# Four-layer graph network on one core: row-tile pairs of the second sweep set twice as far apart, and the last rows stored in one transfer from ScalarE's queue

## The chip, the cores and the metric

The kernel runs on one core of one Trainium2 chip. The metric is the device time of one execution in microseconds (us). Before the change it is 2903.23 us, the median of three runs (2901.61 to 2905.91). The profiled execution has a span of 2899.2 us.

## What is computed

Four layers of a graph network, each followed by a residual and a layer norm. `x` is 2708 x 512, `adj` is a sparse-valued but densely stored 2708 x 2708 matrix with non-negative entries. Cut to what matters here:

```python
deg = jnp.maximum((adj != 0).astype(jnp.float32).sum(-1), 1.0)
x = _layernorm(x + _L0_gnn_ref(x, adj))                    # weighted mean over neighbours
x = _layernorm(x + _L1_gnn_ref(x, adj, adj, ...))          # attention and a plain convolution
x = _layernorm(x + _L2_gnn_ref(x, adj, L2_gnn_weight))     # three hops
x = _layernorm(x + _L3_gnn_ref(x, adj, deg[..., None], L3_gnn_W, L3_gnn_b))

def _L1_gnn_ref(x, adj_a, adj_b, W_sa, a_sa, W_gcnb, b_gcnb, Wa, ba, Wb, bb):
    ...
    x_b = adj_b @ (x @ W_gcnb) + b_gcnb                    # the second sweep
    return jax.nn.sigmoid(attn_a * x_a + attn_b * x_b)

def _L3_gnn_ref(x, adjacency, node_degree, W, b):
    a_hat = adjacency + jnp.eye(n)
    dinv = jax.lax.rsqrt(node_degree)
    pooled = (dinv * a_hat * dinv) @ x + x
    return jax.nn.relu(pooled @ W + b)                     # dinv * dinv is 1 / degree, by rows
```

## The kernel before

Seven sweeps over the adjacency matrix make up the kernel; each is a product of `adj` with 512 columns of features. Products are cut into two halves in each direction and done with seven block products instead of eight (P1 to P7). `at(pos, fn)` puts a piece of work into a list at a position, and the list is emitted in the order of positions; a scheduler then lays out the instructions of each engine with this order as priority. In a sweep over `RANGES` a step of 1.0 is one block product, and a range takes seven steps.

```python
RANGES = [(0, 384), (384, 384), (768, 256), (1024, 330)]
PLAIN = dict(P1=0, P7=1, P5=2, P6=3, P4=4, P3=5, P2=6)      # where each block product starts
RING = 38
...
    def bank(nm, shape=None):                               # eight PSUM banks for everything
        return psum.tile(shape or [P, D], F32, name=nm, tag="x", bufs=8)
...
    def move(queue, dst, src):                              # rows in a multiple of 16, then the others
        m = dst.shape[0]
        c = m - m % 16 if m > 16 else m
        queue.dma_start(out=dst[:c], in_=src[:c])
        if c < m:
            queue.dma_start(out=dst[c:m], in_=src[c:m])
```

In the second sweep the rows of a finished range go through a dense product with `W_gcnb`, again in seven block products, tile by tile. `seven` does it in two parts. Part 0 fills the blocks u, c and d of two PSUM banks, and VectorE adds u, c and d to the outputs. Part 1 fills a and accumulates further products into u, c and d, so it has to wait until VectorE has read what part 0 left there.

```python
    def seven(part, Y, wop, H, lo, w, outs, scales, bases):
        if part == 0:
            x, y = bank("ps_7"), bank("ps_7")
            H.update(u=x[:, :HD], c=x[:, HD:], d=y[:, :HD], a=y[:, HD:])
        for home, a, v in SEV[part]:                        # three homes in part 0, four in part 1
            for c in range(2):
                nc.tensor.matmul(H[home][:w], Y[a, c][:, lo : lo + w], wop(v, c), ...)   # L644
        def acc(i, e, home, first=False):
            ...
                nc.vector.tensor_tensor(o, H[home][:w], b, ALU.add)                      # L651
        if part == 0:
            acc(0, 0, "u", True)
            acc(1, 1, "c", True)
            acc(1, 1, "d")
        else:
            acc(0, 0, "a")
            for i, e in ((1, 1), (0, 1), (1, 0)):
                acc(i, e, "u", (i, e) != (1, 1))
            acc(1, 0, "c")
            acc(0, 1, "d")
...
        # in done1, for every range but the last; p0 is step 7.12 of the range,
        # which is step 0.12 of the next one
        at(p0 + 0.3, lambda: Y.update(row_sums(...)))       # six new tiles of the ring
        for i, (t, lo, w) in enumerate(tiles):              # 3, 3 and 2 tiles of 128 rows
            ...
            at(p0 + 0.6 + 0.56 * i, lambda f=b7: f(0))
            at(p0 + 0.6 + 0.56 * i + 0.26, lambda f=b7: f(1))
```

While this happens, the next range runs: its block products (L457), the sums of adjacency tiles that they read (L402), the count of the degrees (L963), with `end(1)` (bank `ds`) at step 2.6 and `rows(1)` (bank `ps_r`) at step 3.2, and the attention scores (L900 to L916).

The last layer ends with `done6`. For the last group of rows it handles six tiles in a row, the last of them with 83 rows:

```python
            def b(s=s, lo=lo, w=w, r0=r0, got=got):
                px = dense(lambda c: cc(s, c)[:, lo : lo + w], W[6], w)                        # L605
                y = got["x"]
                ...
                nc.vector.scalar_tensor_tensor(px[:w], px[:w], rdeg_f[...], vec[6][:w], ...)   # L1479
                nc.vector.scalar_tensor_tensor(y[:w], px[:w], 0.0, y[:w], ALU.max, ALU.add)    # L1480
                layernorm([(y, 0, D)], y, w, True)          # L554 to L564, its end on ScalarE
                move(nc.sync, out[h * NH + r0 : h * NH + r0 + w, :], y[:w])                    # L151, L153
```

Of the kernel before, what the change touches and what calls it, by code (L numbers as in the profile page):

```python
# [27 lines left out]
NH = 1354  # L28
# [40 lines left out]
def gnn_kernel(ctx: ExitStack, tc: tile.TileContext, x, adjT, w_sa, a_sa, w_gcn, b_gcn, wab, bab, w_hop, w_out,  # L69
               b_out, out):  # L70
    nc = tc.nc
# [75 lines left out]
    def move(queue, dst, src):  # L147
# [6 lines that stand above are left out]
# [7 lines left out]
    def trans(nm):  # L161
        return pool.tile([P, 384], F32, name=nm, tag="ring", bufs=RING)

    def nat(nm):
        return pool.tile([P, D], F32, name=nm, tag="nat", bufs=6)
# [4 lines left out]
    def bank(nm, shape=None):  # L170
        return psum.tile(shape or [P, D], F32, name=nm, tag="x", bufs=8)
# [6 lines left out]
    def at(pos, fn, hold=False):  # L178

        def go():  # L180
            n = len(nc.cur_bb.bb.instructions)
            fn()
            held.update(range(n, len(nc.cur_bb.bb.instructions)))

        events.append((pos, len(events), go if hold else fn))
# [413 lines left out]
    def dense(lhs, wts, w):  # L599
        ps = bank("ps_d")  # L600
        for c in range(DC):
            for n in range(len(wts) // DC):
                r = wts[c] if len(wts) == DC else wts[2 * c + n]
                o = ps[:w] if len(wts) == DC else ps[:w, n * HD : (n + 1) * HD]
                nc.tensor.matmul(o, lhs(c), r, start=c == 0 and n == 0, stop=c == DC - 1, skip_group_check=True)  # L605
        return ps
# [16 lines left out]
    def row_sums(A, n):  # L623

        Y = {("A11", c): A[0, c] for c in range(2)}
        Y.update({("A12", c): A[0, 2 + c] for c in range(2)})
        Y.update({("A22", c): A[1, 2 + c] for c in range(2)})
        for c in range(2):
            for m, a, b, op in (("S3", A[0, c], A[1, c], ALU.subtract), ("S1", A[1, c], A[1, 2 + c], ALU.add),
                                ("S2", None, A[0, c], ALU.subtract), ("S4", A[0, 2 + c], None, ALU.subtract)):  # L630
                Y[m, c] = A[1, c] if m == "S1" else ring_tile("d7")
                a = Y["S1", c] if a is None else a
                b = Y["S2", c] if b is None else b
                nc.vector.tensor_tensor(Y[m, c][:, :n], a[:, :n], b[:, :n], op)
        return Y
# [6 lines that stand above are left out]
        for home, a, v in SEV[part]:  # L642
            for c in range(2):
                nc.tensor.matmul(H[home][:w], Y[a, c][:, lo : lo + w], wop(v, c),  # L644
                                 start=part == 0 and home in "ud" and c == 0, stop=c == 1, skip_group_check=True)

        def acc(i, e, home, first=False):
            o = outs[i][:w, e * HD : (e + 1) * HD]
            b = bases[i][:w, e * HD : (e + 1) * HD] if first else o
            if scales is None:  # L650
                nc.vector.tensor_tensor(o, H[home][:w], b, ALU.add)  # L651
            else:
                nc.vector.scalar_tensor_tensor(o, H[home][:w], scales[i], b, ALU.mult, ALU.add)
# [11 lines that stand above are left out]
# [182 lines left out]
    for k in range(KW):  # L847
        f = k / KT
# [89 lines left out]
    i = 0  # L938
# [55 lines left out]
    def done1(p0, dp, last, R0, n, h, C, tiles):  # L994
        Z = {}

        def gates():

            pg = bank("pg")
            for c in range(DC):  # L1000
                nc.tensor.matmul(pg[32 * c : 32 * c + 32, :n], wab_pad[:, c, :], C[h, c][:, :n], start=True, stop=True)
            Z[0] = trans("zg")
            nc.scalar.copy(Z[0][:, :n], pg[:, :n])

        def gate_tile(i, t, lo, w):
            if i == 0:
                Z[1] = bank("pz", [P, 8])
            pz = Z[1][:, 2 * i : 2 * i + 2]
            nc.tensor.matmul(pz[:w], Z[0][:, lo : lo + w], pick, start=i == 0, stop=True, skip_group_check=True)
            nc.vector.tensor_tensor(gate[:w, t, :], pz[:w], gate_x[:w, t, :], ALU.add)  # L1010
            nc.scalar.activation(gate[:w, t, :], gate[:w, t, :], AF.Sigmoid)

        def finish(t, w, y):
            nc.scalar.mul(y[:w], y[:w], gate[:w, t, 1:2])
            move(nc.gpsimd, XB[t], y[:w])

        at(p0 + 0.05, gates)
        for i, (t, lo, w) in enumerate(tiles):
            def b(i=i, t=t, lo=lo, w=w):
                gate_tile(i, t, lo, w)  # L1020
                if not last:
                    return
                px = dense(lambda c: C[h, c][:, lo : lo + w], W[1], w)
                y = nat("y")
                nc.vector.tensor_tensor(y[:w], px[:w], vec[1][:w], ALU.add)
                finish(t, w, y)

            at(p0 + 0.25 + (dp * i if last else 0.02 * i), b)
        if last or h:
            return  # L1030

        Y = {}
        at(p0 + 0.3, lambda: Y.update(row_sums({(i, c): C[1 - i, c] for i in range(2) for c in range(DC)}, n)))
        for i, (t, lo, w) in enumerate(tiles):
            H, y = {}, []

            def b7(part, t=t, lo=lo, w=w, H=H, y=y):
                if part == 0:
                    y.extend(nat("y") for _ in range(2))
                seven(part, Y, W[8], H, lo, w, y, None, [vec[1], vec[1]])  # L1040
                if part == 1:
                    for j in range(2):
                        finish(t + KT * (1 - j), w, y[j])

            at(p0 + 0.6 + 0.56 * i, lambda f=b7: f(0))
            at(p0 + 0.6 + 0.56 * i + 0.26, lambda f=b7: f(1))

    sweep(S[1], RANGES, extra=extra1, done=done1, late=0.85, save=True)

    eps_col = const.tile([P, NT], F32, name="eps_col")  # L1050
# [112 lines left out]
    def fetch2(src, h, r0, w):  # L1163
        o = nat("ld")
        for t, a, b, m in split(h, r0, w):
            move(nc.gpsimd, o[b : b + m, :], src[t][a : a + m, :])
        return o
# [297 lines left out]
    def done6(p0, dp, g, i0, n, h, cc, tiles):  # L1465

        end = (g, h) == (1, 0)
        for i, (s, lo, w) in enumerate(tiles[3:] + tiles[:3] if end else tiles):
            got = {}
            r0 = i0 + s * n + lo  # L1470

            def a(r0=r0, w=w, got=got):
                got["x"] = fetch2(X3, h, r0, w)

            def b(s=s, lo=lo, w=w, r0=r0, got=got):
                px = dense(lambda c: cc(s, c)[:, lo : lo + w], W[6], w)
                y = got["x"]
                r = 12 * g + 6 * h + 3 * s + lo // P
                nc.vector.scalar_tensor_tensor(px[:w], px[:w], rdeg_f[:w, r : r + 1], vec[6][:w], ALU.mult, ALU.add)  # L1479
                nc.vector.scalar_tensor_tensor(y[:w], px[:w], 0.0, y[:w], ALU.max, ALU.add)  # L1480
                layernorm([(y, 0, D)], y, w, True)
                move(nc.sync, out[h * NH + r0 : h * NH + r0 + w, :], y[:w])

            p = p0 - 0.095 + 0.14 * i if end else p0 + 0.1 + 0.28 * i
            at(p - 0.6, a)
            at(p, b)
# [57 lines left out]
```

## Time and profile before

| | |
|---|---|
| time, median of 3 runs | 2903.23 us |
| span of the profiled execution | 2899.2 us |
| VectorE busy | 2241.0 us (77%) |
| GpSimd busy | 626.6 us (22%) |
| mean DMA rate | 176 GB/s |
| second sweep | about 500 to 900 us |
| dense product of the second sweep (L644) | 554.0 to 788.3 us, 224 instructions of 0.379 us |
| last matrix product ends | about 2888.6 us |

Engines have short names in the profile: PE is TensorE's matrix product, PEld its loading of weights, DVE is VectorE, ACT ScalarE, POOL GpSimd, SP SyncE; a q behind a name means the engine's queue of orders. L644 is line 644 of the kernel. A line of a timeline gives the start, the length, the engine, the line, the operation, the tiles out and in, the shape and the number of instructions merged in it; brackets at its end hold the idle time before it and what ended it. A row of waits gives who waited, for what, how long in total, how often and the longest. A single-precision product shows as two instructions.

### The profile page before, as it was taken

Reading aid. Unit: us, or ns where it says so; the run is one execution under the profiler, and the core shown is the slowest. Engines: PE = TensorE matmul, PEld = TensorE weight load, DVE = VectorE, ACT = ScalarE, POOL = GpSimd, SP = SyncE. Lnnn points to the kernel's source line nnn. Section 1 sums busy time; section 2 is a strip of 40 time slices with the busy share of each in tenths; the row PEclk is TensorE's granted clock in tenths of the full one; section 3 lists DMA queues with packets and bytes.
Section 4 is the critical chain, followed back from the end, with each engine's and each line's share of the span. In section 5 each row is a group of like instructions: output and inputs, shape, how many; then the busy total and the mean of one; then the engine's idle time right before and its main releaser. Section 6 shows DMA issues by size and latency. Waiting matters only on the chain. (4 is left out here: it accounts for less than half of the span.)

```text
span 2899.2 us, 37366 instructions
## 1 busy us (share of the span) xinstructions
PE 2844.7 (98%) x10847; PEld 1852.6 (64%) x10847; DVE 2241.0 (77%) x5778; ACT 566.7 (20%) x1110; POOL 626.6 (22%) x1133
## 2 busy tenths in 40 slices
PE   7999999999999999999999999999999999999998
PEld 5655665657765656866666666666666666665664
DVE  6898798577748675875689788887888878798776
ACT  4544200001137454651100000000000100100001
POOL 0123224123310101122213033030330212501102
PEclk9999999999999999999999999999999999999999
DMA  7666466354544333564667667566675665764551
GB/s 228 190 211 180 132 211 228 108 173 152 172 150 128 118 115 96 171 197 151 202 208 226 204 197 235 171 205 204 198 234 167 196 187 171 237 172 142 173 154 59
DMA packets 373145, 511.50 MB, mean 176 GB/s; under 512 B 64022, under 2 KB 326096, under 8 KB 372940
## 3 DMA queue, kind: packets, MB, share of 16 engines
q1 hardware_dynamic: 307128, 372.01, 44.1%
q0 software_dynamic: 50272, 127.29, 12.9%
q10 hardware_dynamic: 15540, 9.82, 1.2%
q8 instruction: 86, 1.41, 0.2%
q14 instruction: 119, 0.97, 0.1%
HBM read 425.22 MB, written 83.67 MB: 176 GB/s over the span
## 5 line engine op out<-in xcount | busy, mean ns | idle before, releaser
L1218 DVE TENSOR_TENSOR z<-z 128x339 f32<-128x339 f32 (+1 forms) x966 | 456.0, 505 | 11.7 <-PE accu L1271 3.4
L1289 ACT COPY q<-accu 128x338 f32<-128x338 f32 (+1 forms) x84 | 34.5, 443 | 1024.0 <-PE accu L1271 1024.0
L559 POOL TENSOR_TENSOR rstd<-rstd,neg_half 128x1 f32<-128x1 f32 (+3 forms) x92 | 59.2, 644 | 722.9 <-DVE rstd L558 717.2
L1271 PE MATMUL accc<-s,t 128*128 128x338 f32 (+1 forms) x644 | 198.2, 452 | 0.0
L1271 PE MATMUL accu<-z,t 128*128 128x338 f32 (+1 forms) x644 | 194.4, 448 | 0.6 <-DVE z L1218 0.6
L1271 PE MATMUL accc<-z,t 128*128 128x338 f32 (+1 forms) x644 | 193.7, 448 | 0.0
L1271 PE MATMUL accd<-z,t 128*128 128x338 f32 (+1 forms) x644 | 193.6, 448 | 0.0
L1402 POOL DMA_DIRECT2D Y<-y x192 | 104.8, 552 | 376.2 <-DVE y L1397 342.7
L402 DVE TENSOR_TENSOR a<-a,a 128x384 f32<-128x384 f32 (+2 forms) x330 | 162.6, 514 | 11.0 <-PE accu L457 10.3
L1271 PEld LDWEIGHTS accc<-s,t 128*128 128x128 f32 x644 | 121.5, 191 | 65.8 <-issue 8.9
L1271 PEld LDWEIGHTS accc<-z,t 128*128 128x128 f32 x644 | 122.0, 190 | 61.6 <-issue 2.2
L1271 PEld LDWEIGHTS accd<-z,t 128*128 128x128 f32 x644 | 122.2, 190 | 61.3 <-issue 1.5
L1271 PEld LDWEIGHTS accu<-z,t 128*128 128x128 f32 x644 | 121.7, 190 | 61.8 <-issue 2.1
L1218 DVE TENSOR_TENSOR s<-z 128x338 f32<-128x338 f32 (+1 forms) x322 | 150.2, 505 | 8.2 <-PE accc L1271 7.4
L1295 DVE TENSOR_TENSOR q<-q,accd 128x338 f32<-128x338 f32 (+1 forms) x112 | 56.4, 503 | 126.7 <-PE accd L1271 126.7
L1072 ACT ACTIVATE e<-row,neg_s 128x384 f32<-128x384 f32 (+5 forms) x176 | 100.4, 570 | 81.0 <-DVE e L1074 28.9
L1073 ACT ACTIVATE f<-row,neg_s 128x384 f32<-128x384 f32 (+5 forms) x176 | 100.0, 568 | 26.5 <-PE accc L457 7.1
L1074 DVE TENSOR_TENSOR e<-e,f 128x384 f32<-128x384 f32 (+5 forms) x176 | 87.8, 508 | 21.0 <-ACT f L1073 20.1
L963 DVE SCALAR_TENSOR_TENSOR deg<-a,deg 128x384 f32<-128x384 f32 (+2 forms) x152 | 75.0, 505 | 14.7 <-DMA a<-in_adjT 13.9
L605 PE MATMUL ps_d<-w,q 128*128 128x512 f32 (+2 forms) x192 | 85.7, 593 | 0.0
L1075 DVE SCALAR_TENSOR_TENSOR a<-a,e 128x384 f32<-128x384 f32 (+2 forms) x160 | 80.4, 509 | 3.0 <-DMA a<-in_adjT 0.7
L405 POOL DMA_DIRECT2D As<-a x120 | 64.9, 544 | 80.3 <-DVE a L402 70.0
(651 smaller groups left out, 5899.4 us busy)
## 6 DMA issues: line engine op xcount, KB each, us to landing
z<-As SPq DMA_DIRECT2D x320, 169.5 KB
z<-As SPq DMA_DIRECT2D x320, 169.0 KB
a<-in_adjT SPq DMA_DIRECT2D x240, 192.0 KB
z<-in_adjT SPq DMA_DIRECT2D x240, 169.5 KB
z<-in_adjT SPq DMA_DIRECT2D x240, 169.0 KB
a<-in_adjT SPq DMA_DIRECT2D x120, 165.0 KB
a<-in_adjT SPq DMA_DIRECT2D x112, 128.0 KB
As<-a POOLq DMA_DIRECT2D x60, 192.0 KB, 3.9
```

Source lines behind the costliest of these rows:

```text
L402: nc.vector.tensor_tensor(A[r, dst, k][:, :n], A[r, a, k][:, :n], A[r, b, k][:, :n], op)
L405: nc.gpsimd.dma_start(out=SD[m][k * P : (k + 1) * P, R0 : R0 + n], in_=A[r, dst, k][:, :n])
L559: nc.gpsimd.tensor_tensor(rstd[:w, 1:2], rstd[:w, 0:1], neg_half[:w], ALU.pow)
L605: nc.tensor.matmul(o, lhs(c), r, start=c == 0 and n == 0, stop=c == DC - 1, skip_group_check=True)
L963: nc.vector.scalar_tensor_tensor(d[:w, :n], a[:w, :n], 0.0, d[:w, :n], ALU.not_equal, ALU.add)
L1072: nc.scalar.activation(e[:w, :n], row[R0, h][0][:w, :n], AF.Exp, bias=neg_s[:w, t : t + 1])
L1073: nc.scalar.activation(f[:w, :n], row[R0, h][1][:w, :n], AF.Exp, bias=neg_s01[:w, t : t + 1])
L1074: nc.vector.tensor_tensor(e[:w, :n], e[:w, :n], f[:w, :n], ALU.min)
L1075: nc.vector.scalar_tensor_tensor(a[:w, :n], a[:w, :n], 0.0, e[:w, :n], ALU.not_equal, ALU.mult)
L1218: nc.vector.tensor_tensor(d[:, :n], Z[x + (k,)][:, :n], Z[y + (k,)][:, :n], op)
L1271: nc.tensor.matmul(B[home][:, :n], stat(v, k), a[:, :n], start=bool(start and k == 0), stop=k == nk - 1, skip_group_check=True)
L1402: nc.gpsimd.dma_start(out=rows[:, :, f * P : (f + 1) * P], in_=o[32 * f : 32 * (f + 1), : m * P].rearrange("p (b d) -> p b d", d=P))
```

## The change

The first edit sets the row tiles of the second sweep's dense product 1.1 steps apart instead of 0.56, and the two parts of a tile 0.5 instead of 0.26. VectorE has more time between part 0 and part 1, and the work of the dense product is spread more evenly over the next range. The second edit stores the last 83 rows of the output in one transfer that ScalarE issues itself, right behind the instruction that makes these rows. It saves the second transfer of 3 rows and the hand-over from ScalarE to SyncE. No arithmetic changes.

```diff
-            at(p0 + 0.6 + 0.56 * i, lambda f=b7: f(0))
-            at(p0 + 0.6 + 0.56 * i + 0.26, lambda f=b7: f(1))
+            at(p0 + 0.6 + 1.1 * i, lambda f=b7: f(0))
+            at(p0 + 0.6 + 1.1 * i + 0.5, lambda f=b7: f(1))
 ...
-            def b(s=s, lo=lo, w=w, r0=r0, got=got):
+            def b(i=i, s=s, lo=lo, w=w, r0=r0, got=got):
                 px = dense(lambda c: cc(s, c)[:, lo : lo + w], W[6], w)
 ...
                 layernorm([(y, 0, D)], y, w, True)
-                move(nc.sync, out[h * NH + r0 : h * NH + r0 + w, :], y[:w])
+                o = out[h * NH + r0 : h * NH + r0 + w, :]
+                if end and i == 5:
+                    nc.scalar.dma_start(out=o, in_=y[:w])
+                else:
+                    move(nc.sync, o, y[:w])
```

## The prediction

> **What bounds the kernel now.** I read the page's first part, then the waits of TensorE, then its timeline at the place that the first edit moves, and last the end of the run.
>
> The shares of the whole span:
>
> ```profile
> PE 2844.7 (98%) x10847; PEld 1852.6 (64%) x10847; DVE 2241.0 (77%) x5778; ACT 566.7 (20%) x1110; POOL 626.6 (22%) x1133
> ```
>
> TensorE (PE) is busy for 2844.7 of 2899.2 us, and the change neither adds nor removes a matrix product. All that a new order can win is PE's idle time: 54.5 us in all, of which 16.0 lie in the first 50 us and 11.45 in the last 40 (the table by stretches). The first edit acts in the second sweep, which lies between 500 and 900 us. There PE's waits are two rows (waiter, what it waited for, us in total, times, longest):
>
> ```profile
> PE ps L644 <- DVE y L651: 2.3, 3, 1.1
> PE pg L1001 <- DVE C L518: 1.5, 1, 1.5
> ```
>
> L644 is the matrix product in `seven`, the one whose calls are moved; L651 is VectorE (DVE) adding an unscaled block out of PSUM. So at most a few microseconds are there for the taking. PE's own timeline shows where (start, length, and in brackets the idle time before):
>
> ```profile
> 582.80 0.59 PE L644 MATMUL ps<-T2D,P1c 128*128 128x256 f32 x2
> 583.24 1.45 PE L457 MATMUL accc<-s,T3D 128*128 128x384 f32 x4
> 584.53 1.45 PE L457 MATMUL accd<-a,T1A 128*128 128x384 f32 x4
> 587.12 0.70 PE L644 MATMUL ps<-T3D,d 128*128 128x256 f32 x2 [1.14 <-DVE y L651]
> 587.92 1.13 PE L644 MATMUL ps<-w,W 128*128 128x256 f32 x4
> ```
>
> Part 0 of the third row tile ends here at about 583.2, eight instructions of the sweep follow, and part 1 then stands still: it writes into the PSUM columns that DVE has not read yet. DVE is late because the sums `a<-a,a`, the degree counts and a run of small score operations stand ahead in its queue.
>
> Now the end of the run:
>
> ```profile
> 2892.39 0.81 ACT L564 ACTIVATE ld<-ld,rstd 83x512 f32<-83x512 f32 x1 [2.63 <-DVE rstd L561]
> 2893.23 0.33 SPq L151 DMA_DIRECT2D out<-ld  x1
> 2893.68 0.27 SPq L153 DMA_DIRECT2D out<-ld  x1
> ```
>
> ScalarE finishes the last 83 rows at 2893.20; SyncE issues 80 rows at 2893.23 and the other 3 at 2893.68. The closing drains, instructions of the kernel's last lines (number, then length in ns as shortest, median and longest, then first and last start), show what holds the end at 2899.2:
>
> ```profile
> L1540 POOLq DRAIN  x3: 46/106/6872, 2891.5 to 2898.9; - x3
> L1540 SPq DRAIN  x3: 7/7/7, 2895.3 to 2898.7; - x3
> ```
>
> SyncE, which waits for the stores, is through at 2895.3. GpSimd's (POOL's) first drain begins at 2891.5 and takes 6.87 us, to 2898.4; only then do the engines meet, and 0.8 us later the program is over. So the stores now have about 3.0 us to spare (2898.4 less 2895.4).
>
> **What the Trainium skill says.** "DMA: Bandwidth & Descriptors", section "Why a DMA increments its semaphore by 16 and not by 1": the number of engines k that carry a transfer is the largest number up to 16 that divides the slowest dimension of both access patterns; the page's example is 127 partitions on one engine. 83 is prime, so by this page the new store runs on one engine. The trace agrees as far as it can: the store of 3 rows is followed by one semaphore update at once and by three as its data land, where the 80-row store has sixteen landings. No transfer of a prime number of rows over 16 is in the kernel before, because its helper `move` cuts at a multiple of 16.
>
> The same page, "Issuing engines are not separate DMA queues": transfers issued from the scalar, sync and GpSimd queues use the same 16 engines. So the scalar queue brings no engines of its own; it can save only time at the issue. The trace shows how little that is: 0.03 us lie between ScalarE's end and SyncE's issue.
>
> "Perfetto Trace Analysis", section "Tensor Engine Instruction (MATMUL, LD_WEIGHTS)": PE's ends are a model and not observed. I therefore checked the stalls by the distance between starts. A 384-column instruction is normally 0.323 us before the next, a 256-column one 0.216. The excess over these at the third tile of the first range is 1.30 and 0.27 us, at the third tile of the second range 1.00 and 0.47; the third range, which has two tiles, has none. This agrees with the waits and is a little more: 3.04 us.
>
> **The change part by part.** First edit. No instruction is added. Part 1 of a tile moves from 0.26 to 0.50 of a step behind part 0, and tiles from 0.56 to 1.10 apart. A step is ten k tiles, each four PE instructions of 0.323 us, so 12.9 us in the 384-column ranges. The gap between the parts grows from 0.26 x 12.9 = 3.4 us of sweep work to 6.5 us. The lateness of DVE at the two bad places was 1.57 us (1.30 + 0.27) and 1.47 us, less than the 3.1 us that each gap gains in the 384-column ranges; the second bad place runs inside the 256-column range, where a step is 8.6 us and the gap gains 2.1 us. Both stalls should go: -3.0 us.
>
> Against that stand three costs. The third tile now begins at 2.92 and ends at 3.42 steps into the next range, where before it ended at 2.10. It holds two of eight PSUM banks, while by then the sums u, c and d hold six; the bank of the degree count (`ds`, 2.6) must be free before the third tile starts, and the turned degrees (`ps_r`, 3.2) must come after it. Each may put DVE's latency in front of PE once in the two ranges with three tiles: I take 0.5 us a piece for the first, the size of the small waits seen above, so +1.0. Next, the six ring tiles of row sums are held some 1.3 steps longer, and the loads of the sweep live on free ring slots. With 10+10+10 tiles in use, 6 of row sums and 2 of remaining rows the 38 are full already up to step 2, in the kernel before too; after that the sums of step 1 to 2 have let go of ten, so I count nothing. Last, about 6 us of PE work moves from before product P5 (step 2.0) to behind it, so that its sums must be ready 6 us sooner; DVE has 3.8 us less to do by then (nine adds of 0.42 us). Here I count nothing but keep it as a risk. First edit together: -2.0 us.
>
> Second edit. It removes one issue (0.27 us plus 0.12 before it) and one hand-over. It moves 83 x 2,048 = 169,984 bytes from 16 engines to one. In the stretch 2890.60 to 2891.40, which is the store of the tile before, the DMA share is 0.85 and the rate 328 GB/s, so a busy engine moves 328 / (16 x 0.85) = 24.1 GB/s. The packet records say the same: 2,048 bytes take 81 to 84 ns, and packets of one engine follow 80 ns apart. The 83 rows therefore take 6.6 to 7.0 us on one engine, where five rows an engine take 0.4.
>
> From 2893.25 (issue) the first packet leaves 0.85 us later, as for the earlier stores; I add 0.2 because stores and loads that run on few engines took longer to issue (0.55 to 0.6 us for the copies of 32 rows against 0.33). That is 2894.3; plus 6.7 is 2901.0; plus 0.35 to landing, as in the 128-row store, is 2901.35. SyncE needs about 0.3 to get through its last semaphores, and 0.75 from there to the end as now: 2902.4, against 2899.2. The second edit costs +3.2 us, as the 3.0 us to spare swallow the first half of the delay.
>
> Sum: -2.0 + 3.2 = +1.2 us if GpSimd's drain is independent of the stores.
>
> **The rivals.** (a) GpSimd's long drain is not a fixed length but ends some time after other things end. Then nothing is to spare and the store costs its whole 6.2 us: -2.0 + 6.2 = +4.2. Its start right at the last GpSimd instruction and its end at no other event speak for a fixed length; but there is one such drain only. (b) The store is spread over 16 engines after all. Then the removed issue falls into the slack, and the change is worth the first edit alone, -2 to -3 us. That this helper cuts everywhere at 16 speaks against it. (c) The later tiles upset the sweep: product P5 waits for sums, or loads wait for ring slots. DVE already waits 13.9 us in this stretch for loads of the adjacency (14 times), and these waits could grow and reach PE: +2 to +6 us more. (d) The instruction order is laid out anew beyond the moved calls, and small waits appear or go elsewhere: 1 to 2 us either way.
>
> **Range and chances.** Weighing +1.2 (six in ten), +4.2 (a quarter) and -2.5 (one in ten), and a little for (c), I take +1.7 us over 2903.2: 2904.9 us. The runs of before differ by 4.3 us among themselves (2901.61 to 2905.91), and the risks add some 3 us, more of it upward: 2900.5 to 2909.5. Two per cent are 58 us; nothing here is of that size: within 2% 0.985, faster 0.005, slower 0.01.
>
> **What would show it.** Right: no row of PE waiting for L651 between 500 and 900 us, 2 to 3 us less PE idle time there; at the end one store from ScalarE's queue, after which the DMA share is about 1/16 (0.06) with some 25 GB/s for nearly 7 us; SyncE's drain at about 2901.6 less what the sweep has won, later than GpSimd's. Wrong: a short burst of over 150 GB/s at the end; GpSimd's drain lengthened; a PE wait for `ds`, `ps_r` or the sums of P5 of more than 1 us; or PE's idle time changed elsewhere by more than the second sweep won.

## The result and the profile after

The changed kernel takes 2915.39 us (median of 4 runs, 2911.55 to 2917.45), the kernel before 2903.52 us beside it (4 runs): a ratio of 1.0039, with a 95% interval of 1.0022 to 1.0056, that is +6 to +16 us. It is slower, but within 2%. The predicted 2904.9 us and its range to 2909.5 us were missed upwards.

The busy times of the page of the changed kernel are those of before, within 3 us:

```profile
PE 2845.7 (98%) x10847; PEld 1854.0 (64%) x10847; DVE 2243.5 (77%) x5778; ACT 566.2 (19%) x1110; POOL 627.1 (22%) x1133
```

The span grew from 2899.2 to 2913.2 us, so what came is waiting. In the list of PE's waits over the whole span (who waited, for what, us in total, times, longest), L644 no longer stands, and two rows are new:

```profile
PE ds L977 <- DVE y L651: 5.6, 2, 4.2
...
PE ps_r L921 <- DVE y L651: 3.7, 3, 2.1
```

The part 1 that stood still has gone, as it was meant to. But PE now waits for the same adds of VectorE (L651) at other products: the degree count `ds` (L977) and the turned score and degree rows `ps_r` (L921). None of these reads what L651 writes. What they need is a PSUM bank. PE's timeline after the second tile of the first range:

```profile
585.08 1.03 PE L644 MATMUL ps<-w,d 128*128 128x256 f32 x4
585.95 1.45 PE L457 MATMUL accd<-a,T1B 128*128 128x384 f32 x4
589.48 0.27 PE L921 MATMUL ps_r<-ident,rcol 128*6 128x128 f32 x1 [2.08 <-DVE y L651]
```

The tile is done for PE at 586; a few products later comes one that takes a bank, and it waits until VectorE has emptied the tile's banks. The worst place is the last range. VectorE's timeline there, and PE's from the same stretch:

```profile
795.50 0.48 DVE L963 SCALAR_TENSOR_TENSOR deg<-a,deg 128x330 f32<-128x330 f32 x1
799.66 0.50 DVE L963 SCALAR_TENSOR_TENSOR deg<-a,deg 128x330 f32<-128x330 f32 x1 [3.67 <-DMA a<-in_adjT]
801.65 0.50 DVE L963 SCALAR_TENSOR_TENSOR deg<-a,deg 128x330 f32<-128x330 f32 x1 [1.49 <-DMA a<-in_adjT]
802.36 0.50 DVE L963 SCALAR_TENSOR_TENSOR deg<-a,deg 128x330 f32<-128x330 f32 x1 [0.21 <-DMA a<-in_adjT]
802.78 0.42 DVE L651 TENSOR_TENSOR y<-ps,y 128x256 f32<-128x256 f32 x1
803.11 0.74 DVE L651 TENSOR_TENSOR y<-ps,vec 128x256 f32<-128x256 f32 x2
803.77 1.07 DVE L651 TENSOR_TENSOR y<-ps,y 128x256 f32<-128x256 f32 x3
```

```profile
796.02 1.02 PE L644 MATMUL ps<-w,d 128*128 128x256 f32 x4
796.88 1.27 PE L457 MATMUL accd<-a,T1B 128*128 128x330 f32 x4
797.99 2.38 PE L457 MATMUL accd<-a,T1C 128*128 128x330 f32 x8
804.57 1.26 PE L977 MATMUL ds<-ones_f,deg 128*128 128x1 f32 x6 [4.20 <-DVE y L651]
```

The six adds of the tile could have begun at 797. Ahead of them in VectorE's queue stand four counts of degrees, and the adjacency tiles of three of these are still being loaded; VectorE waits 3.67, 1.49 and 0.21 us for them, and PE waits for VectorE. The table by stretches then shows what follows such a wait (us, busy time and number of instructions of the engines, granted clock of PE, DMA share, GB/s):

```profile
799.00:804.50 5.50, 1.38 (x5) 0.59 (x4) 3.15 (x9) 0.00 (x0) 0.00 (x0) 0.92 0.94 331
804.50:811.00 6.50, 6.43 (x17) 4.55 (x18) 4.74 (x19) 1.33 (x2) 2.62 (x5) 0.54 0.68 214
811.00:818.00 7.00, 7.00 (x28) 4.71 (x27) 3.52 (x7) 0.26 (x1) 3.20 (x6) 1.00 0.43 132
```

From 803.6 to 810.4 us, that is for 6.8 us, the granted clock is half. In the first 1.0 us of this PE still waits; then products that are 0.28 us apart otherwise are 0.55 us apart, which costs another 3.1 us (the sum of the excesses over the usual distance). The Trainium skill has this in "TensorE: Matmul & The Clock Gate", section "Part 1: The HAM clock gate (the "warmup" mystery)": an idle window of about 3.4 us puts PE on half clock, and a busy one of that length lifts it. The trace agrees in the length: half clock comes within the 4.2 us of waiting and lasts 6.83 us, twice 3.41. It does not agree that a whole window has to be idle; what the traces show instead stands in the last section.

The end of the run. ScalarE's last instruction and the store that follows it:

```profile
2902.66 0.81 ACT L564 ACTIVATE ld<-ld,rstd 83x512 f32<-83x512 f32 x1 [2.63 <-DVE rstd L561]
2903.51 0.28 ACTq L1484 DMA_DIRECT2D out<-ld  x1
```

The stretch after it, in the same columns as above, and the closing drains (number; shortest, median and longest in ns; first and last start):

```profile
2905.00:2911.00 6.00, 0.00 (x0) 0.00 (x0) 0.00 (x0) 0.00 (x0) 0.00 (x0) 0.50 0.07 23
```

```profile
L1544 POOLq DRAIN  x3: 46/106/6872, 2901.8 to 2913.0; - x3
L1544 SPq DRAIN  x3: 7/7/7, 2912.4 to 2912.7; - x3
```

A DMA share of 0.07 is about one engine of sixteen, at 23 GB/s. The store's semaphore shows it too: it is updated once at 2903.95 us and has one landing, at 2912.25, where the 80-row store of before has sixteen. GpSimd's drain takes 6.872 us, to the nanosecond what it took before, and ends at 2908.7; SyncE is through with the stores only at 2912.4. From the end of ScalarE's last instruction to the end of the span it is 9.75 us, where it was 6.00.

The sum, from the starts of the same PE instructions in the two traces: the changed kernel is 1.15 us ahead just before the moved calls (at 550 us) and 6.8 us behind after the last range (870 us), so the second sweep costs 8.0 us. At the end of ScalarE's last instruction it is 10.3 us behind, and at the end of the span 14.0: 3.7 us more. The 3.5 us between 870 us and the end of the products are not the change's: the order of instructions is the same there, and the profiles of e2, e3, e6 and e7 (below), whose order of PE is that of before throughout, are 3.3 to 5.1 us behind over the same stretch. The largest part is a wait and half clock in the third layer that vary from run to run. A part of the difference of 14.0 is also the profile of before, whose run took 2901.01 us, near the lowest of its runs.

### The profile page after: what moved, and what is told of

Read it like the earlier page. It is cut to its first block, busy times and chain, and to the rows that moved or that the text cites. A ratio compares the mean times of both kernels' runs of the same rounds, so it can differ in the third digit from the quotient of the medians.

```text
span 2913.2 us, 37368 instructions
## 1 busy us (share of the span) xinstructions
PE 2845.7 (98%) x10847; PEld 1854.0 (64%) x10847; DVE 2243.5 (77%) x5778; ACT 566.2 (19%) x1110; POOL 627.1 (22%) x1133
```

## The experiments

**Each edit alone.** Edit one is the change's first hunk, edit two its second.

```diff
 e1_pairs:  only
-            at(p0 + 0.6 + 0.56 * i, lambda f=b7: f(0))
-            at(p0 + 0.6 + 0.56 * i + 0.26, lambda f=b7: f(1))
+            at(p0 + 0.6 + 1.1 * i, lambda f=b7: f(0))
+            at(p0 + 0.6 + 1.1 * i + 0.5, lambda f=b7: f(1))
 e2_store:  only
+                if end and i == 5:
+                    nc.scalar.dma_start(out=o, in_=y[:w])
+                else:
+                    move(nc.sync, o, y[:w])
```

> The first edit alone (row-tile pairs 1.1 and 0.5 steps apart), the end as before. Theory M (the middle): PE waits for a PSUM bank that a row tile still holds, because VectorE has not yet done the tile's last adds; two waits of about 2 us at the degree count (ds) and one of 4.4 us in the last range, which is followed by two stretches of half clock (6.8 us at half speed). The profile pair puts +8 us there: about 2911 us, with PE waits for L651 of about 9 us. Rival T (the end): the whole loss of 12 us belongs to the last store; then this kernel takes 2901 to 2903 us. Rival C (chance): the middle differs from run to run; then the time lies anywhere from 2901 to 2912 with a wide interval.

Measured: 2912.36 us against 2903.96 us, ratio 1.0037 (1.0024 to 1.0049). PE's waits between 500 and 900 us are again only two rows:

```profile
PE ds L977 <- DVE y L651: 5.9, 2, 4.4
PE ps_r L921 <- DVE y L651: 4.5, 3, 2.3
```

So the larger part of the loss is the first edit's, and rival T falls. That rival C is not needed is seen from the interval and from the same two rows with nearly the same numbers.

> The second edit alone (83 rows in one transfer from ScalarE's queue), pairs as before. Theory M: one engine carries 83 x 2,048 bytes in 6.7 us; about 3 us of that lie behind GpSimd's drain of 6.87 us, so +3.7 us: about 2907 us; from the end of ScalarE's last instruction to the end of the span 9.7 us instead of 6.0. Rival T: +12 us, about 2915 us. Had the drain moved with the store: +6.5 us.

Measured: 2909.55 us, ratio 1.0020 (1.0011 to 1.0029), that is +3.2 to +8.4 us; the trace has 9.74 us from ScalarE's last instruction to the end, 3.7 more than before. GpSimd's drain is again 6.872 us long. The trace's 3.7 us lie inside the interval. Together the two ratios make 1.0057, the change has 1.0039, and their intervals overlap.

**Is it the queue or the cut?** The same rows in one transfer from SyncE, and in two from ScalarE, pairs as before.

```diff
 e3_sync_one:
-                    nc.scalar.dma_start(out=o, in_=y[:w])
+                    nc.sync.dma_start(out=o, in_=y[:w])
 e6_scalar_two:
-                    nc.scalar.dma_start(out=o, in_=y[:w])
+                    move(nc.scalar, o, y[:w])
```

> Pairs as before; the last 83 rows in one transfer, but from SyncE's queue. Theory M (one engine because 83 is prime): 9.7 us from ScalarE's last instruction to the end of the span, as with ScalarE's queue, and some 25 GB/s at the end. Rival Q (ScalarE's queue is the slow part): 6.0 us, as before.

> Pairs as before; the last rows from ScalarE's queue, cut into 80 and 3. Theory M: 6.0 us from ScalarE's last instruction to the end, no gain, because GpSimd's drain covers the stores either way. Rival Q: 9 us or more.

Measured, one run each: 9.72 us from ScalarE's last instruction to the end with one transfer from SyncE, 6.00 us with two from ScalarE. The two drain rows of the first and then of the second:

```profile
L1544 POOLq DRAIN  x3: 46/106/6873, 2895.0 to 2906.1; - x3
L1544 SPq DRAIN  x3: 7/7/7, 2905.6 to 2905.9; - x3
```

```profile
L1544 POOLq DRAIN  x3: 46/106/6872, 2897.3 to 2904.7; - x3
L1544 SPq DRAIN  x3: 7/7/7, 2901.1 to 2904.4; - x3
```

With one transfer SyncE is through 3.7 us after GpSimd's drain (2895.0 + 6.87 = 2901.9), with two 3.0 us ahead of it (2904.2). The queue does nothing; the single transfer of 83 rows does all. The saved hand-over is worth nothing, because the drain covers it.

**Is the drain the end's bound?** In the kernel before, the inverse root of the last tile's variance is taken off GpSimd.

```diff
 e7_last_pow:  in layernorm, for the last tile only
-        nc.vector.tensor_scalar(rstd[:w, 0:1], mv[:w, 1:2], EPS, None, ALU.add)
-        nc.gpsimd.tensor_tensor(rstd[:w, 1:2], rstd[:w, 0:1], neg_half[:w], ALU.pow)
+            nc.vector.tensor_scalar(c, mv[:w, 1:2], EPS, None, ALU.add)
+            nc.scalar.activation(q, c, AF.Sqrt)
+            nc.vector.reciprocal(q, q)
+            nc.vector.tensor_tensor(t, q, q, ALU.mult)
+            nc.vector.scalar_tensor_tensor(t, c, -0.5, t, ALU.mult, ALU.mult)
+            nc.vector.scalar_tensor_tensor(rstd[:w, 1:2], t, 1.5, q, ALU.add, ALU.mult)
```

The run also takes one square root on ScalarE at the first of the last six tiles, whose result is not used.

> Pairs and stores as before; the inverse root of the last row tile is taken by ScalarE and VectorE (square root, reciprocal, one Newton step) in place of GpSimd, whose last instruction so comes one tile (3.4 us) earlier. Theory M (the drain is a fixed 6.87 us and sets the end): the drain ends 3.4 us earlier, the stores set the end, which comes 2 to 3 us earlier less 0.5 us for the longer chain: about -2 us, 2902 us. Had the drain waited for the stores: no gain, 0 to +0.5 us.

```profile
L1554 POOLq DRAIN  x3: 46/106/6875, 2892.0 to 2900.2; - x3
L1554 SPq DRAIN  x3: 7/7/7, 2899.6 to 2899.9; - x3
```

In the trace it is as expected: the drain keeps its length and ends at 2898.9, ahead of SyncE at 2899.6, and the end comes 2.99 us after ScalarE's last instruction instead of 6.00, while the chain before it is 0.33 us longer. So the drain is a fixed length that starts with GpSimd's last instruction, and it set the end before. On the clock the 2.7 us do not show: 2904.22 us against 2904.27, ratio 0.9999 (0.9991 to 1.0007; the interval reaches to -2.6 us). Whether something takes the gain back stays open. PE's order is that of before, yet its last product begins at 2891.9 us in this profile and at 2888.0 in that of before: single profiles of the same order differ by more than the gain.

**Which range, and what in it?** The first edit only where there are three tiles:

```diff
 e4_pairs_two:
+            d, e = (1.1, 0.5) if len(tiles) > 2 else (0.56, 0.26)
-            at(p0 + 0.6 + 1.1 * i, lambda f=b7: f(0))
-            at(p0 + 0.6 + 1.1 * i + 0.5, lambda f=b7: f(1))
+            at(p0 + 0.6 + d * i, lambda f=b7: f(0))
+            at(p0 + 0.6 + d * i + e, lambda f=b7: f(1))
```

> The first edit only in the two ranges with three row tiles; the third range (two tiles, whose pairs run inside the last range) keeps 0.56 and 0.26. Theory M: the wait of 4.4 us and the half clock after it (6.3 us together in the profile pair) are gone; the smaller waits in the other ranges (5.7 us against 3.0 before) stay: +1.5 to +3 us, about 2905.5 us. Rival R (ring): the row sums hold six ring slots longer and make loads late in every range; then two thirds of the loss stay: +5 us or more.

Measured: 2904.45 us, ratio 1.0004 (0.9995 to 1.0012); `ds` has one wait of 1.4 us left, `ps_r` its three (4.4 us). So most of the loss of the first edit is made in the last range, though the waits for the tiles of the other two are as many. The ring as the cause in every range falls.

Then the first edit whole, and the bank's takers moved behind the last tile, in the last range only:

```diff
 e8_ds_last:
-        at(pb + 2.6, lambda: end(1))
-        at(pb + 3.2, lambda: rows(1))
+        at(pb + (3.5 if r == 3 else 2.6), lambda: end(1))
+        at(pb + (4.6 if r == 3 else 3.2), lambda: rows(1))
```

> The first edit; only in the last range are the degree count (ds) and the turned degrees (ps_r) moved behind the last pair's adds (steps 3.5 and 4.6 instead of 2.6 and 3.2). VectorE still waits for its loads there. Theory M (the wait is for the bank): the wait of 4.4 us at ds and the half clock after it are gone, so the time falls to that with the third range's pairs left alone: 2904 to 2907 us. Rival R (VectorE is late because of the loads, and PE will wait elsewhere for it): 2910 us or more, with a PE wait of over 3 us at another product of the last range.

Measured: 2905.53 us, ratio 1.0004 (0.9996 to 1.0012). No PE wait above 0.2 us is left in the last range, and no half clock. The row sums hold their ring slots as long as in the first edit alone, and VectorE waits as long for loads as in the changed kernel: 20.5 us between 500 and 900 us against 20.0, where the kernel before has 13.9. The six adds of the last tile begin 5.7 us after its last product ends, just as in the changed kernel, and yet PE does not wait for them: rival R falls here too. Whether it is the ring that makes VectorE's waits for loads longer stays open; buffers of their own for the row sums were not tried.

The sharpest one leaves PE's order and the banks as the first edit has them, and only reorders VectorE's queue in the last range: the degree counts of the late-loaded quarter are held behind the adds.

```diff
 e12_held_tally:  with the first edit; a third argument keeps the work behind all emitted before it
-                at(pb + p + 0.8 * k / KT, lambda ij=ij, k=k: tally(int(ij[0]) - 1, (ij, k)))
+                at(pb + p + 0.8 * k / KT, lambda ij=ij, k=k: tally(int(ij[0]) - 1, (ij, k)), r == 3 and ij == "12")
```

> The first edit, ds and ps_r where they were; only VectorE's order in the last range differs: the degree counts of the late-loaded quarter (12) are held behind the adds of the last row tile, of which four stood ahead of them. PE's order is that of the first edit alone. Theory M2 (the bank that ds takes is released by adds that stand in VectorE's queue behind counts whose loads are still under way): the wait of 4.4 us at ds and the half clock go, 2904 to 2907 us. Rival B (the bank alone, at the ordinary pace of VectorE): the wait at ds stays above 3 us and the time near 2912 us.

VectorE's adds come at once now, and PE's stretch from the tile to `ds` has no gap:

```profile
796.28 1.31 DVE L402 TENSOR_TENSOR a<-a,a 128x330 f32<-128x330 f32 x3
797.67 0.42 DVE L651 TENSOR_TENSOR y<-ps,y 128x256 f32<-128x256 f32 x1
798.01 0.75 DVE L651 TENSOR_TENSOR y<-ps,vec 128x256 f32<-128x256 f32 x2
798.67 1.07 DVE L651 TENSOR_TENSOR y<-ps,y 128x256 f32<-128x256 f32 x3
```

```profile
799.44 2.38 PE L457 MATMUL accd<-a,T1C 128*128 128x330 f32 x8
801.66 0.64 PE L977 MATMUL ds<-ones_f,deg 128*128 128x1 f32 x6
802.15 1.36 PE L457 MATMUL accd<-a,T1C 128*128 128x330 f32 x4
```

Measured: 2906.4 us against 2903.54, ratio 1.0009 (1.0001 to 1.0017), where the first edit alone has 1.0037. The granted clock is 1.00 from 792 to 818 us. This settles the cause in the last range: `ds` takes a bank that six adds must first empty, and these stood behind counts whose loads were under way. What is left, 1.0009, fits the smaller waits for the tiles of the other two ranges (5.8 us in the rows of waits, where those of before have 2.3), which no run took away alone.

**Two attempts that did not do what they should.** With the first edit, `ds` and `ps_r` were moved in all ranges:

```diff
 e5_late_deg:
-        at(pb + 2.6, lambda: end(1))
-        at(pb + 3.2, lambda: rows(1))
+        at(pb + 3.9, lambda: end(1))
+        at(pb + 4.2, lambda: rows(1))
```

> The first edit, and the degree count's bank (ds) and the turning of the degrees (ps_r) moved from steps 2.6 and 3.2 to 3.9 and 4.2, behind the last pair. Theory M: no product has to take a bank that a tile has just used, so PE no longer waits for L651 at ds and ps_r, and the 3.0 us that the pairs of before lost are gone too: -2 to -3 us, about 2901 us. Rival R (ring): loads are as late as before and VectorE with them, so PE waits at other products: +4 to +8 us.

Measured: 2908.63 us, ratio 1.0017 (1.0010 to 1.0023). The waits at `ds` are gone, but the expected gain is not there. The time lies where rival R put it, but the waits do not have rival R's reason. PE's waits between 400 and 900 us:

```profile
PE ps_n L588 <- DVE P1c L518: 4.4, 1, 4.4
PE ps_r L921 <- DVE rdeg L983: 3.3, 1, 3.3
PE ps_r L921 <- DVE y L651: 2.1, 1, 2.1
```

The first row belongs to the sweep before and stands in every profile of this kernel (3.3 to 4.4 us). The second is this edit's own fault: `ps_r` came too close behind its degrees, in the first range. The third is a score row that nothing moved. After both waits PE runs at half clock for 3.4 us (0.57 in the stretch from 499 to 503 us, 0.66 from 594 to 599). Two waits and two such stretches make about 3.3 + 2.1 + 2 x 1.7 = 8.8 us, less the 3.0 us of the old stalls and 1.5 of a wait at L1001 that is not in this profile: +4.3, near the measured +4.7.

A smaller gap that ends each tile before the sum d takes its banks, alone and with the last inverse root off GpSimd:

```diff
 e11_gap, and e10_both with e7_last_pow's edit:
-            at(p0 + 0.6 + 0.56 * i, lambda f=b7: f(0))
-            at(p0 + 0.6 + 0.56 * i + 0.26, lambda f=b7: f(1))
+            at(p0 + 0.6 + 0.5 * i, lambda f=b7: f(0))
+            at(p0 + 0.6 + 0.5 * i + 0.36, lambda f=b7: f(1))
```

> Stores as before; tiles 0.5 of a step apart and the parts 0.36, so that the last tile still ends (2.08) before the sum d takes its banks. Theory M2: the two stalls of before (3.0 us) shrink to about 0.5 us and ds and ps_r wait for no row tile: -1 to -3 us, 2902 us. If widening the gap between the parts is harmful in itself: 2907 us or more.

> That gap together with the last inverse root taken off GpSimd. Theory M2: -1 to -3 us from the pairs and -2.7 us from the end: about 2900 us. If neither shows beyond the spread of the runs: 2904 us.

Measured: 2903.29 us, ratio 0.9999 (0.9990 to 1.0007), and 2904.07 us, ratio 1.0000 (0.9992 to 1.0008). In the trace of the first, PE's waits at the moved work are down to 0.6 us at L644 and 0.7 us at `ps_r`, and there is no wait at `ds`; but neither kernel beats the one before by anything that can be measured. In the trace of the second, a wait of 2.3 us at the product of L1001, which is not of these edits, is followed by 7 us at a clock of 0.52, which takes more than the edits give. Counted by the starts of the same PE instructions, as in the sum further up, from before the moved calls to 870 us, the second sweep is 8.7 us longer than before in the profile of e1, 1.4 to 1.6 in e4, e8 and e12, 3.9 in e5 and 1.8 in e10, and 2.1 us shorter in e11. The four profiles with the order of before (e2, e3, e6, e7) lie 0.1 to 1.2 us below it, so one such count is good to about 1 us. No version found here is measurably faster than the kernel before.

## Why the prediction was wrong

**Second edit: right in mechanism, 0.5 us short.** One engine for 83 rows, 3.0 us swallowed by GpSimd's drain, the drain of a fixed length: each is shown (e2, e3, e6, e7). Predicted was +3.2 us, measured 3.7. The term that was too small is the transfer: 6.6 to 7.0 us were worked out from packets 80 ns apart; the 83 packets leave within 7.5 us, as their distance is 80 ns in the median but 92 in the mean. The 0.2 us added for a slower issue were not needed (the issue took 0.28 us, and the first packet left 0.8 us after its start), which hid a part of this. Of the rivals, (a) and (b) fall.

**First edit: the sign was wrong.** Predicted -2.0 us, measured +8.4 alone. Three steps failed.

First, "Both stalls should go: -3.0 us" was right as far as it went: L644 waits no longer. But what PE waited for, VectorE's adds, is still late, and PE meets it again one step on, at whatever next takes a bank. The prediction named `ds` and `ps_r` for this and then put "0.5 us a piece" on them, "the size of the small waits seen above". That size was taken from the waits of part 1, not from how long VectorE needs to empty a tile. Measured by the distances between starts are 2.2, 0.9, 1.5 and 1.0 us for the tiles of the first two ranges, 5.7 us in all where 1.0 was put down (the rows of waits have 5.1); the first of the four is a turned score row, which was not on the list at all.

Second, the cost was counted "in the two ranges with three tiles" and none in the last range. Its second tile ends at step 2.32, before `ds` at 2.6, and this looked safe. The trace of before shows that it was not: VectorE's queue at that place waits four times, 3.6 us in all, for adjacency loads, between 795 and 803 us:

```profile
DVE deg L963 <- DMA a<-in_adjT: 3.6, 4, 1.3
```

Before the change the last adds of the tile came ahead of them, so these waits cost nothing:

```profile
792.20 0.75 DVE L651 TENSOR_TENSOR y<-ps,y 128x256 f32<-128x256 f32 x2
```

The change moved the adds behind them. Rival (c) had named the waits, the "13.9 us in this stretch for loads", and they did grow, to 20.0 us; but it stood at the edge of the weighing, and the 6 us of its upper end would have made +4.0 of the first edit, not +8.4.

Third, PE's clock was left out. A wait was counted as long as it lasts. The wait of 4.2 us in the last range cost 7.3 us, since half clock follows. The kernel before showed such stretches in its own trace (0.84 in the mean from 1526 to 1537 us, after a wait of 2.6 us). With this the parts add up: 7.3 + 5.7 - 3.0 for the stalls that went, less 1.7 for a wait at L1001 that the profile of before has and this one has not, make 8.3 us, near the 8.0 us by which the second sweep grew.

Rival (d) is real as spread, not as an effect of the change: the wait in the third layer was 2.6 us in the profile of before, 3.8 in e2 and 4.4 in e3, e6 and e7, whose PE order is the same, and 4.0 after. What the prediction said would prove it wrong, a PE wait for `ds` or `ps_r` of more than 1 us, is what was found. One reading was off without effect: PE's idle time in the last 40 us is 10.7 us and not 11.45, as the stretch reached 0.8 us past the end.

## What to carry to other kernels

Moving work later to spare one wait moves everything that it holds, here two of eight PSUM banks: list what takes such a buffer next, and read in the profile what stands ahead of the releasing instruction in its engine's queue, loads above all. Count a TensorE wait of two microseconds or more with the half clock that may follow (3.4 or 6.8 us of it here), not by its length alone. Before joining two stores into one, look at the number of rows: 80 and 3 took 3.7 us less to the end than 83 at once. And look for what already covers the end before saving an issue there.

## What was not expected

GpSimd's closing drain took 6.872 to 6.877 us in every trace, from its last instruction on, whatever the stores did; it hides 3.0 us of them. A transfer of 83 rows of 2,048 bytes on one engine has its packets leave over 7.5 us, at 23 GB/s, from either queue.

PE's half clock follows the idle time within one stretch of 3.41 us, not the length of a wait. In each of the 13 traces the changes of the granted clock lie on a grid of 3.41 us. Cut on this grid from 100 us to the last product, with PE idle where no product is recorded, the traces have 41 stretches at full clock with 1.9 us or more of idle time, and half clock followed all 41. It followed 3 of the 27 with 1.5 to 1.9 us and none of the 10,489 with less. So a wait of 2.3 us at L1001 in e10, of which 2.05 us fell into one stretch, brought half clock, and one of 2.4 us at the same product in e2, which was split (1.64 us at most in one stretch), did not. Half clock went on for another stretch after all 11 stretches at half clock with 0.5 us or more of idle time, and after 1 of the 45 with less than 0.3 us. The wait of 4.2 us fell into two stretches, with 3.23 and 0.97 us, and brought two at half clock. The ends of products are modelled in the profile, so these limits are rough.
